# A graph layer on one core: the first group's second layer moved ahead, and the last three node blocks in an order written by hand

## The chip, the cores and the metric

The kernel runs on one core of a Trainium2 chip. The metric is the device time of one execution in microseconds (us), as the median of several runs. A core has five engines with a queue each: TensorE (PE, with its weight loads as PEld), VectorE (DVE), ScalarE (ACT), GpSimd (POOL) and SyncE (SP), which here only issues transfers.

## The reference, cut to what matters

There are 6250 nodes with 128 features and 100,000 edges, sorted by destination. Each edge passes a network of three layers, the messages are averaged over each node's incoming edges, each node passes a network of two layers, and the result is normalized.

```python
msg_in = concatenate([x[src], x[dst]], axis=-1)              # 100000 x 256
h = relu(msg_in @ Wm1 + bm1)                                 # 256 hidden
h = relu(h @ Wm2 + bm2)
messages = h @ Wm3 + bm3                                     # 128
agg = segment_sum(messages, dst) / clip(count, 1.0)[:, None]
upd = relu(concatenate([x, agg], axis=-1) @ Wn1 + bn1) @ Wn2 + bn2
y = x + (x + upd)
out = (y - mean(y)) / sqrt(var(y) + 1e-5)                    # over the 128 features
```

## The kernel before

The work has three stages. In all of them the arithmetic is in float32 (the destination half of the first edge layer is held as three bfloat16 terms).

**Tables (to about 84 us).** The products of all nodes with the two halves of `Wm1` are written to tables in DRAM, one half for sources (`atab`), one for destinations (`btab`). `x_part` (lines 316 to 320) computes the node features' own share of the later node layer, per block of 512 nodes as two products `c = 1, 0` of 512 columns, and lets ScalarE or VectorE empty each bank with the bias added. Blocks 9 and 12 are kept back for the edge stage (`X_FIRST`); block 12 is the short one, 106 nodes.

**Edges (84 to about 1129 us).** The loop runs over 196 groups of 512 edges (the last is shorter). For group g, POOL gathers rows of `atab` by source (`ag`, line 412, four buffers), SP loads windows of `btab` (`bw`, line 418), and

- `first_layer` (lines 449 to 460): TensorE transposes the gathered rows into two PSUM banks `ph` (tile pool `p1`, two buffers) and adds the destination share by a product with a 0/1 matrix `oht`, which VectorE compares out of the destinations (line 433); ScalarE applies bias and ReLU to both banks in four steps and so makes `h1`.
- `second_layer` (lines 469 to 471): sixteen matmul records on `h1` into two banks `ph2` (pool `p2`, two buffers), each emptied by VectorE with a `max` into `h2`. The products of `x_part` in this stage use the same two banks of `p2`.
- `sums` and `add_up` (lines 478 to 494): the sums by destination within a group are added to `acc` in SBUF.

One turn of the loop issues, for the group g that is due: `add_up` of group g - 4, `first_layer` of g, in the first two turns also the tests of the next group (`make_hot`) and one block of `x_part`, then `sums` of g - 3 and `second_layer` of g - 1. The order on TensorE is the order of the program (`manual_schedule`), and for the first six turns of the loop that of VectorE and ScalarE is too. So TensorE's order at the start of the stage is: first layer 0, block 9, first layer 1, block 12, second layer 0, first layer 2, second layer 1.

**Nodes (1131 us to the end).** The nodes are cut into 15 blocks: the last 106 nodes first, then blocks of 512, and at either end two of 256. `products` (line 671) multiplies `acc` by `Wm3` and POOL divides by the counts. `hidden` (lines 685 to 687) makes the hidden layer `u`. `norm` (lines 698 to 723) multiplies by `Wn2` into `pot` (two banks), adds twice the features, loaded by SP into `x2`, to give `y` (line 703, two buffers), takes the moments of each 128 nodes with `bn_stats` and `bn_aggr` (lines 707 and 708), the root on ScalarE (`sd`, 710), the reciprocal and the shift on VectorE (`rs` 712, `sh` 714), and scales `y` to `o` on ScalarE, 128 nodes an instruction (718). SP stores `o`. Blocks run four ahead for `products` and two behind for `norm`. TensorE's order is that of the program; VectorE's and ScalarE's order is a scheduler's.

Of the kernel before, what the change touches and what calls it, by code (L numbers as in the profile page):

```python
# [9 lines left out]
F32 = mybir.dt.float32  # L10
BF16 = mybir.dt.bfloat16
I32 = mybir.dt.int32
AF = mybir.ActivationFunctionType
ALU = mybir.AluOpType
AX = mybir.AxisListType
ENG = mybir.EngineType
# [3 lines left out]
P = 128  # L20
# [7 lines left out]
def kernel(  # L28
# [36 lines left out]
    nc = tc.nc  # L65
    N, D = x.shape
# [5 lines left out]
    NG = -(-E // GE)  # L72
# [78 lines left out]
    with tc.tile_pool(name="prep", bufs=1) as prep, tc.tile_pool(  # L151
        name="brow", bufs=6
    ) as brow, tc.tile_pool(name="pp", bufs=3, space=PSUM) as pp, tc.tile_pool(
        name="pb", bufs=5, space=PSUM
# [240 lines left out]
    with edge, tc.tile_pool(name="wk", bufs=2) as wk, tc.tile_pool(  # L395
        name="p1", bufs=2, space=PSUM
# [135 lines left out]
        for i in range(NG + ahead + 1):  # L532
            if i == 6:
                turns.close()
            if i == 16:
                late_loads()
                none = wk.tile([16, (NG * GE - E) // 16], I32, name="none", bufs=1)
                nc.vector.memset(none, NONE)
                nc.sync.dma_start(dpad[:E].rearrange("(p e) -> p e", p=16), dst.rearrange("(p e) -> p e", p=16))
                nc.sync.dma_start(dpad[E:].rearrange("(p e) -> p e", p=16), none)  # L540
            for step, after in enumerate((20, 24, 27)):
                if i >= after and (i - after) % 8 == 0 and (i - after) // 8 < len(pieces):
                    double((i - after) // 8, step)
            if i < NG:
                nt = GT if i < NGF else LT
                firsts = load_bases(tilei[0:1, i * GT:(i + 1) * GT], nt, ENG.SP)
                if i == NGF:
                    dbs = last_destinations()
                elif i % 2 == 0:
                    dbs = early.pop(0) if early else destinations(i, min(2, NGF - i), dst_row)  # L550
                st[i] = dict(nt=nt, got=fetch(srcT[:, i, :], nt, firsts), db=dbs.pop(0))
            g = i - ahead
            if 0 <= g < NG:
                s = st[g]
                ag, bw = s.pop("got")

                def make_hot(g):
                    s = st[g]
                    hots[g], s["oh"] = hot(s.pop("db"), pbase[:, g, :], dloc[:, g, :s["nt"]], s["nt"])

                if g not in hots:
                    make_hot(g)
                oht = hots.pop(g)
            k = g - lag - 1
            if 0 <= k < NG:
                s = st.pop(k)
                if "firsts" not in s:
                    s["firsts"] = load_bases(tilei[0:1, k * GT:(k + 1) * GT], s["nt"], ENG.DVE)
                add_up(s["part"], s["firsts"], s["nt"])
            if 0 <= g < NG:  # L570
                s = st[g]
                s["h1"] = first_layer(ag, bw, oht, s["nt"])
                if first:

                    make_hot(g + 1)
                    whole(x_part(first.pop(0), bank_p2, (nc.scalar, nc.vector)))
            k = g - lag
            if 0 <= k < NG:
                s = st[k]
                s["part"] = sums(s["oh"], s["h2"], s["nt"])  # L580
            m = g - 1
            if 0 <= m < NG:
                s = st[m]
                s["h2"] = h2s[m % NH2]
                second_layer(s["h1"], s["h2"], s["nt"])
# [59 lines left out]
    with tc.tile_pool(name="nd", bufs=2) as nd, tc.tile_pool(name="nr", bufs=1) as nr, tc.tile_pool(  # L645
        name="pm", bufs=4, space=PSUM
    ) as pm, tc.tile_pool(name="pu", bufs=2, space=PSUM) as pu, tc.tile_pool(
        name="po", bufs=2, space=PSUM
    ) as po, tc.manual_schedule(engines={ENG.PE}):


        rcol = nr.tile([P, NC], F32, name="rcol")
        nc.sync.dma_start(rcol, acc[0:1, HC, :NT * P].rearrange("o (p n) -> o p n", n=NC))
        nc.vector.tensor_scalar_max(rcol, rcol, 1.0)
        nc.vector.reciprocal(rcol, rcol)
        nc.sync.dma_start(rtab.rearrange("(p n) -> p n", n=NC), rcol)
        rrow = rtab.rearrange("(o n) -> o n", o=1)

        def products(b):

            n0, n1 = nodes_of[b]
            w = n1 - n0
            rc = nd.tile([P, NB], F32, name="rc", bufs=6)
            if b < SELF:
                nc.vector.tensor_scalar_max(rc[:, :w], acc[:, HC, n0:n1], 1.0)  # L665
                nc.vector.reciprocal(rc[:, :w], rc[:, :w])  # L666
            else:
                nc.sync.dma_start(rc[:, :w], rrow[:, n0:n1].to_broadcast([P, w]))
            pmt = pm.tile([P, NB], F32, name="pmt")
            for c in range(HC):  # L670
                nc.tensor.matmul(pmt[:, :w], w3[:, c, :], acc[:, c, n0:n1], start=(c == 0), stop=(c == HC - 1))  # L671
            total = nd.tile([P, NB], F32, name="total", bufs=3)
            nc.vector.scalar_tensor_tensor(total[:, :w], acc[:, HC, n0:n1], b23, pmt[:, :w],  # L673
                                           op0=ALU.mult, op1=ALU.add)
            agg = nd.tile([P, NB], F32, name="agg", bufs=5)
            nc.gpsimd.tensor_mul(agg[:, :w], total[:, :w], rc[:, :w])  # L676
            return agg

        def hidden(b, agg):
            n0, n1 = nodes_of[b]  # L680
            w = n1 - n0
            u = nd.tile([P, HC, NB], F32, name="u", bufs=4)
            for c in range(HC):
                put = pu.tile([P, NB], F32, name="put")
                nc.tensor.matmul(put[:, :w], wu1[:, 1, c * P:(c + 1) * P], agg[:, :w], start=True, stop=True)  # L685
                nc.vector.tensor_add(u[:, c, :w], put[:, :w], xu[c][:, n0:n1])  # L686
                nc.scalar.activation(u[:, c, :w], u[:, c, :w], AF.Relu)  # L687
            return u

        def norm(b, u):  # L690
            n0, n1 = nodes_of[b]
            w = n1 - n0
            k = -(-w // P)
            r = min(P, w)
            pot = po.tile([P, 4, D], F32, name="pot")
            for i in range(k):
                for c in range(HC):
                    nc.tensor.matmul(pot[:r, i, :], u[:, c, i * P:i * P + r], wu2[:, c, :],  # L698
                                     start=(c == 0), stop=(c == HC - 1))
            x2 = nd.tile([P, 4, D], F32, name="x2", bufs=3)  # L700
            nc.sync.dma_start(x2[:r, :k], x2tab[n0:n1, :].rearrange("(t p) d -> p t d", p=r))
            y = nd.tile([P, 4, D], F32, name="y")
            nc.vector.tensor_add(y[:r, :k, :], x2[:r, :k, :], pot[:r, :k, :])  # L703
            st = nd.tile([P, 4, 6], F32, name="st")
            mv = nd.tile([P, 4, 2], F32, name="mv")
            for i in range(k):
                nc.vector.bn_stats(st[:r, i, :], y[:r, i, :])
                nc.vector.bn_aggr(mv[:r, i, :], st[:r, i, :])
            sd = nd.tile([P, 4], F32, name="sd")
            nc.scalar.activation(sd[:r, :k], mv[:r, :k, 1], AF.Sqrt, bias=eps[:r])  # L710
            rs = nd.tile([P, 4], F32, name="rs")
            nc.vector.reciprocal(rs[:r, :k], sd[:r, :k])  # L712
            sh = nd.tile([P, 4], F32, name="sh")
            nc.vector.scalar_tensor_tensor(sh[:r, :k], mv[:r, :k, 0], -1.0, rs[:r, :k],  # L714
                                           op0=ALU.mult, op1=ALU.mult)
            o = nd.tile([P, 4, D], F32, name="o")
            for i in range(k):
                nc.scalar.activation(o[:r, i, :], y[:r, i, :], AF.Identity, bias=sh[:r, i:i + 1],  # L718
                                     scale=rs[:r, i:i + 1])
            if r == P:  # L720
                nc.sync.dma_start(out[n0:n1, :].rearrange("(t p) d -> p t d", p=P), o[:, :k, :])
            else:
                nc.sync.dma_start(out[n0:n1, :], o[:r, 0, :])

        B = len(nodes_of)
        FORE, BACK = 4, 2
        aggs = {b: products(b) for b in range(FORE)}
        us = {}
        for b in range(B + BACK):
            if b < B:  # L730
                us[b] = hidden(b, aggs.pop(b))
            if b >= BACK:
                norm(b - BACK, us.pop(b - BACK))
            if b + FORE < B:
                aggs[b + FORE] = products(b + FORE)


# [27 lines left out]
```

## Time and profile before

| | |
|---|---|
| median of 3 runs | 1210.17 us (1209.64 to 1211.73) |
| the profiled execution | 1208.8 us |
| its span | 1207.0 us |
| TensorE busy | 1178.5 us, 98% of the span |
| POOL, VectorE, ScalarE busy | 804.9, 670.4, 454.5 us |
| mean granted TensorE clock | 0.996 |
| first group's transposes start | 84.06 us |
| last matmul starts, last scaling starts | 1197.0 us, 1203.6 us |

The span runs from the first to the last instruction that the profiler recorded; the execution's own time lies 1.8 us above it. A row of the timeline merges neighbouring instructions of a kind and gives the start, the time from the first start to the last end, the engine, the line, the operation, the tile written and the tiles read, and in brackets the idle time of the engine before it with what ended it. An instruction's recorded duration includes its way through the engine, so the next one often starts before it ends.

### The profile page before, as it was taken

To read this page: it belongs to the slowest core of one execution; us is meant where nothing else is said; L and a number is where in the kernel's file an instruction comes from. 1 tells how busy PE (TensorE), PEld (TensorE's weight loads), DVE (VectorE), ACT (ScalarE), POOL (GpSimd) and SP (SyncE) were. 2 spreads that over 40 slices of the span, in tenths; PEclk is the share of its full clock that TensorE was granted. 3 is DMA by queue.
4 is the path that set the end of the run, shared out by engine and by line. 5 is a ranking of instruction groups with operands and counts; after the bars stand their busy time and mean duration, and the time that the engine had idled before them with its cause. 6 is when DMAs were issued, how large, how long until landed. Compare 5 with 4: busy or idle time off the path is not lost. (4 is left out here: it accounts for less than half of the span.)

```text
span 1207.0 us, 32797 instructions
## 1 busy us (share of the span) xinstructions
PE 1178.5 (98%) x11196; PEld 895.0 (74%) x11197; DVE 670.4 (56%) x2080; ACT 454.5 (38%) x1163; POOL 804.9 (67%) x859
## 2 busy tenths in 40 slices
PE   7989999999999999999999999999999999999896
PEld 6747777777777777777777777777777777777565
DVE  5864555555555555555555555555555555555586
ACT  5663333333333333333333333333333333333256
POOL 8267777777777777777777777777777777673220
PEclk9999999999999999999999999999999999999999
DMA  8886666666555555555555555555555555552343
GB/s 279 293 261 174 189 180 183 189 191 177 154 151 146 152 153 153 150 152 153 149 148 152 154 154 150 149 152 146 152 153 153 152 152 150 146 148 63 97 111 105
DMA packets 173672, 193.66 MB, mean 160 GB/s; under 512 B 30844, under 2 KB 145486, under 8 KB 173488
## 3 DMA queue, kind: packets, MB, share of 16 engines
q0 software_dynamic: 37984, 103.35, 31.1%
q1 hardware_dynamic: 106956, 61.93, 17.7%
q10 hardware_dynamic: 28564, 26.27, 8.1%
q8 instruction: 90, 1.47, 0.5%
q14 instruction: 78, 0.64, 0.2%
HBM read 168.92 MB, written 22.88 MB: 159 GB/s over the span
## 5 line engine op out<-in xcount | busy, mean ns | idle before, releaser
L412 POOL DMA_INDIRECT ag<-atab,srcT x784 | 752.8, 960 | 282.4 <-issue 184.3
L469 PE MATMUL ph<-w,h 128*128 128x256 f32 x3128 | 727.5, 386 | 1.0 <-ACT x_sb L318 1.0
L469 PEld LDWEIGHTS ph<-w,h 128*128 128x128 f32 x3128 | 578.1, 190 | 152.2 <-DVE acc L494 68.2
L460 ACT ACTIVATE h<-ph,b 128x256 f32<-128x256 f32 x782 | 306.3, 474 | 675.9 <-PE ph L455 495.3
L471 DVE TENSOR_TENSOR h<-ph,nb 128x512 f32<-128x512 f32 x391 | 270.2, 692 | 413.6 <-PE ph L469 411.1
L494 DVE TENSOR_TENSOR acc<-acc,pt 128x63 f32 x782 | 171.7, 220 | 33.9 <-PE ph L455 2.6
L449 PE MATMUL ph<-ident,ag 64*128 64x64 f32 x3128 | 130.3, 223 | 0.6 <-DVE b L382 0.6
L478 PE MATMUL pg<-h,oh 128*32 128x257 f32 x1564 | 125.6, 392 | 0.0
L449 PEld LDWEIGHTS ph<-ident,ag 64*128 64x128 f32 x3128 | 113.5, 139 | 2.7 <-ACT x_sb L318 1.4
L433 DVE TENSOR_SCALAR oht<-db,pbase 128x128 bf16<-128x128 int32 x392 | 104.9, 341 | 1.3 <-PE ph L455 1.0
L489 PEld LDWEIGHTS pt<-ident,part 64*128 64x128 f32 x1173 | 50.9, 136 | 65.9 <-issue 65.2
L455 PE MATMUL ph<-oht,bw 64*128 64x128 bf16 x1564 | 76.6, 217 | 2.7 <-DMA bw<-btab 2.3
L481 ACT COPY part<-pg 128x257 f32<-128x257 f32 x196 | 76.5, 390 | 4.0 <-PE pg L478 4.0
L489 PE MATMUL pt<-ident,part 64*128 64x64 f32 x1173 | 77.8, 238 | 0.2 <-DVE acc L494 0.2
L436 DVE TENSOR_TENSOR oh<-iota_n,dloc 128x128 f32<-128x128 f32 x196 | 55.0, 280 | 20.6 <-PE pg L478 19.7
L676 POOL TENSOR_TENSOR agg<-total,rc 128x512 f32<-128x512 f32 (+2 forms) x15 | 16.0, 1070 | 69.1 <-DVE total L673 65.1
L455 PEld LDWEIGHTS <-bw 64*128 64x128 bf16 x1564 | 53.6, 96 | 3.3 <-DMA bw<-btab 2.6
L232 PE MATMUL pbt<-w,xT 128*128 128x256 f32 x196 | 48.7, 394 | 2.5 <-ACT bt L241 1.6
L478 PEld LDWEIGHTS pg<-h,oh 128*32 128x32 f32 x1564 | 30.8, 108 | 21.7 <-issue 0.8
L232 PEld LDWEIGHTS pbt<-w,xT 128*128 128x128 f32 x196 | 36.8, 197 | 10.9 <-ACT bt L241 2.8
L252 POOL CAST bt<-rest 128x512 bf16<-128x512 f32 x18 | 12.2, 686 | 27.1 <-DVE rest L250 18.0
L698 PEld LDWEIGHTS pot<-wu,u 128*128 128x128 f32 (+1 forms) x196 | 24.0, 191 | 5.5 <-issue 4.8
(109 smaller groups left out, 418.2 us busy)
## 6 DMA issues: line engine op xcount, KB each, us to landing
bw<-btab SPq DMA_DIRECT2D x782, 32.0 KB
db<-in_dst_dram ACTq DMA_DIRECT2D x194, 128.0 KB
ag<-atab,srcT POOLq DMA_INDIRECT x784
btab<-bt SPq DMA_DIRECT2D x24, 384.0 KB
atab<-bt SPq DMA_DIRECT2D x24, 256.0 KB
xd<-in_x_dram SPq DMA_DIRECT2D x12, 256.0 KB
x2tab<-xd SPq DMA_DIRECT2D x12, 256.0 KB
x_sb<-in_x_dram SPq DMA_DIRECT2D x5, 512.0 KB
```

What stands on the lines that cost most here:

```text
L232: nc.tensor.matmul(pbt[:, a, :], xT[:, (t0 + a) * P:(t0 + a + 1) * P], w1[:, k, :], start=True, stop=True)
L412: nc.gpsimd.indirect_dma_start(out=ag[:, j, :], out_offset=None, in_=atab[:, :], in_offset=bass.IndirectOffsetOnAxis(ap=idx[:, j:j + 1], a ...
L433: nc.vector.tensor_scalar(oht[:n, k, :], db[:n, k * P:(k + 1) * P], pb_cols[:n, k:k + 1], None, op0=ALU.is_equal)
L449: nc.tensor.matmul(phs[h][:, c, u * NQ:(u + 1) * NQ], ag[halves[h], u, c * P:(c + 1) * P], ident[halves[h], halves[h]], is_transpose=True, ...
L455: nc.tensor.matmul(phs[h][:, c, k * P:(k + 1) * P], bw[halves[h], k, c * P:(c + 1) * P], oht[halves[h], k, :], start=False, stop=True, ski ...
L460: nc.scalar.activation(h1[:, c, h * 2 * P:(h + 1) * 2 * P], phs[h][:, c, :], AF.Relu, bias=b1[:, c:c + 1])
L469: nc.tensor.matmul(ph2[:, a, :], h1[:, c, (j0 + a) * P:(j0 + a + 1) * P], w2[:, c, :], start=(c == 0), stop=(c == HC - 1))
L471: nc.vector.tensor_tensor(h2[:, j0:j0 + 2, :H], ph2, nb2.to_broadcast([P, 2, H]), op=ALU.max)
L478: nc.tensor.matmul(pg[j * WN:(j + 1) * WN, :], oh[:, j, :], h2[:, j, :], start=True, stop=True, skip_group_check=True)
L481: nc.scalar.copy(part[:n, :], pg[:n, :])
L489: nc.tensor.matmul(pt[:, c, :], rows, ident[halves[h], halves[h]], is_transpose=True, start=True, stop=True, skip_group_check=True)
L494: nc.vector.tensor_add(window, window, pts[j // 2][:, :, k:k + WB])
```

## The change

There are two edits.

In the edge loop, the second layer of group 0 is issued in the turn of group 0 itself, behind the product of block 9; in the next turn it isn't issued again. TensorE's order becomes: first layer 0, block 9, second layer 0, first layer 1, block 12, first layer 2, second layer 1. VectorE's two `max` operations for it move ahead of the tests for group 2. From there on the order is as before.

In the node stage, `norm` is cut into `moments`, `deviation` (the root) and `scaled`. For the blocks up to the twelfth (index 11) they are called one after the other as before. For the last three blocks (12, 13, 14) VectorE and ScalarE follow the order of the program: moments and root of the next block are issued ahead of the scaling of the block before, and some of the scalings go to VectorE as `tensor_scalar` with two operands of one value a partition: the fourth 128 nodes of block 12, the second of block 13, the first of block 14. The tiles `y`, `mv`, `sd` and `o` get three buffers in place of two.

In the changed program VectorE's order from block 12's `y` on is: `y` of 12, `rs` of 11, first `bn_stats` of 12, `sh` of 11, the rest of 12's moments with each `bn_aggr` directly behind its `bn_stats`, `y` and moments of 13, `rs`, `sh` and a scaling of 12, `y` and moments of 14, `rs`, `sh` and a scaling of 13, the same of 14. ScalarE's is: scaling of 11, root of 12, root of 13, three scalings of 12, root of 14, one scaling of 13, one of 14. The order of SP and POOL is unchanged; the stores of the three blocks wait for both engines.

```diff
-            m = g - 1
-            if 0 <= m < NG:
+
+            m = g - 1 if g else g
+            if 0 <= m < NG and "h2" not in st[m]:
                 s = st[m]
                 s["h2"] = h2s[m % NH2]
                 second_layer(s["h1"], s["h2"], s["nt"])
...
-        def norm(b, u):
+        def moments(b, u):
...
-            y = nd.tile([P, 4, D], F32, name="y")
+            y = nd.tile([P, 4, D], F32, name="y", bufs=3)
...
-            mv = nd.tile([P, 4, 2], F32, name="mv")
+            mv = nd.tile([P, 4, 2], F32, name="mv", bufs=3)
             for i in range(k):
                 nc.vector.bn_stats(st[:r, i, :], y[:r, i, :])
                 nc.vector.bn_aggr(mv[:r, i, :], st[:r, i, :])
-            sd = nd.tile([P, 4], F32, name="sd")
+            return y, mv
+
+        def deviation(b, mv):
...
+            sd = nd.tile([P, 4], F32, name="sd", bufs=3)
             nc.scalar.activation(sd[:r, :k], mv[:r, :k, 1], AF.Sqrt, bias=eps[:r])
+            return sd
+
+        def scaled(b, y, mv, sd, engines):
...
-            o = nd.tile([P, 4, D], F32, name="o")
-            for i in range(k):
-                nc.scalar.activation(o[:r, i, :], y[:r, i, :], AF.Identity, bias=sh[:r, i:i + 1],
-                                     scale=rs[:r, i:i + 1])
+            o = nd.tile([P, 4, D], F32, name="o", bufs=3)
+            for i, eng in zip(range(k), engines):
+                if eng is nc.scalar:
+                    eng.activation(o[:r, i, :], y[:r, i, :], AF.Identity, bias=sh[:r, i:i + 1], scale=rs[:r, i:i + 1])
+                else:
+                    eng.tensor_scalar(o[:r, i, :], y[:r, i, :], rs[:r, i:i + 1], sh[:r, i:i + 1],
+                                      op0=ALU.mult, op1=ALU.add)
...
+        for b in range(B - 1):
+            us[b] = hidden(b, aggs.pop(b))
             if b >= BACK:
-                norm(b - BACK, us.pop(b - BACK))
+                y, mv = moments(b - BACK, us.pop(b - BACK))
+                scaled(b - BACK, y, mv, deviation(b - BACK, mv), [nc.scalar] * 4)
             if b + FORE < B:
                 aggs[b + FORE] = products(b + FORE)
+
+        assert BACK == 2
+        with tc.manual_schedule(engines={ENG.DVE, ENG.Activation}):
+            us[B - 1] = hidden(B - 1, aggs.pop(B - 1))
+            ends = [(B - 3, [nc.scalar, nc.scalar, nc.scalar, nc.vector]), (B - 2, [nc.scalar, nc.vector]),
+                    (B - 1, [nc.vector, nc.scalar])]
+            before = None
+            for b, engines in ends:
+                y, mv = moments(b, us.pop(b))
+                sd = deviation(b, mv)
+                if before:
+                    scaled(*before)
+                before = b, y, mv, sd, engines
+            scaled(*before)
```

## The prediction

> **What bounds the kernel now.** I read the page's first two parts, then the timeline around the two places that the diff touches, the chain of the last 17 us, and the granted clock by stretch. First the page:
>
> ```profile
> span 1207.0 us, 32797 instructions
> PE 1178.5 (98%) x11196; PEld 895.0 (74%) x11197; DVE 670.4 (56%) x2080; ACT 454.5 (38%) x1163; POOL 804.9 (67%) x859
> PE   7989999999999999999999999999999999999896
> ```
>
> TensorE is busy from slice 3 to slice 38, so nothing is to be had between: a gain must come from the head, where TensorE waits, or from the tail, where it has finished. The edits touch one of each. The timeline of the head (start, us, what; in brackets the idle time before and what ended it):
>
> ```profile
> 87.80 2.63 PE L316 MATMUL ph<-xT,wu 128*128 128x512 f32 x4
> 87.91 1.57 ACT L460 ACTIVATE h<-ph,b 128x256 f32<-128x256 f32 x4 [4.88 <-PE ph L455]
> 89.35 0.70 ACT L318 ACTIVATE x_sb<-ph,bu 128x512 f32<-128x512 f32 x1
> 90.36 1.11 PE L449 MATMUL ph<-ident,ag 64*128 64x64 f32 x16
> 91.83 0.96 PE L316 MATMUL ph<-xT,wu 128*128 128x106 f32 x4
> 93.37 0.37 ACT L318 ACTIVATE x_sb<-ph,bu 128x106 f32<-128x106 f32 x1
> 93.79 3.72 PE L469 MATMUL ph<-w,h 128*128 128x256 f32 x16 [1.01 <-ACT x_sb L318]
> 97.45 0.72 PE L449 MATMUL ph<-ident,ag 64*128 64x64 f32 x16
> 98.31 3.72 PE L469 MATMUL ph<-w,h 128*128 128x256 f32 x16
> ```
>
> Group 0's second layer (93.79) waits 1.01 us for ScalarE to empty the bank of the small product at 91.83. That wait is what the first edit can remove. From 98.31, the second layer of group 1, both orders are alike, so that start is the yardstick. The clock in stretches (the number before the DMA share is the granted TensorE clock):
>
> ```profile
> 86.00:88.00 2.00, 0.80 (x9) 0.47 (x10) 0.00 (x0) 0.09 (x1) 1.39 (x3) 1.00 0.73 200
> 88.00:90.00 2.00, 2.00 (x4) 0.47 (x3) 0.00 (x0) 2.00 (x5) 1.70 (x2) 0.75 0.84 225
> 90.00:92.00 2.00, 2.00 (x26) 1.45 (x26) 1.34 (x4) 0.12 (x2) 1.39 (x3) 0.50 0.54 158
> 92.00:94.00 2.00, 0.99 (x5) 0.82 (x6) 0.33 (x1) 1.74 (x5) 1.65 (x2) 0.90 0.59 160
> ```
>
> After a stretch in which TensorE waited for transfers the clock is halved, from 89.0 to 92.4 (shares missing: 0.5 of the time at half from 88 to 90, all of it to 92, 0.2 of it to 94, 3.4 us together). The tail's timeline:
>
> ```profile
> 1192.23 0.69 DVE L703 TENSOR_TENSOR y<-x,pot 128x512 f32<-128x512 f32 x1 [0.24 <-issue]
> 1195.34 0.69 DVE L703 TENSOR_TENSOR y<-x,pot 128x512 f32<-128x512 f32 x1 [0.56 <-ACT o L718]
> 1196.50 1.65 ACT L718 ACTIVATE o<-y,sh,rs 128x128 f32<-128x128 f32 x4 [0.70 <-ACT u L687]
> 1198.18 0.42 DVE L703 TENSOR_TENSOR y<-x,pot 128x256 f32<-128x256 f32 x1 [0.83 <-ACT o L718]
> 1200.76 0.42 DVE L703 TENSOR_TENSOR y<-x,pot 128x256 f32<-128x256 f32 x1 [1.34 <-ACT o L718]
> 1203.19 0.88 ACT L718 ACTIVATE o<-y,sh,rs 128x128 f32<-128x128 f32 x2 [0.48 <-DVE sh L714]
> ```
>
> Each `y` of blocks 12, 13 and 14 (1195.34, 1198.18, 1200.76) waits for ScalarE to finish the scaling `o` two blocks earlier, because `y` has two buffers. VectorE and ScalarE work in turn, and the chain of these 17 us gives the scaling 35% of them.
>
> **The sum, against 1208.8 us.** The profiled execution took 1208.8 us, 1.8 us around its span of 1207.0; the median of the three runs, 1210.17, is 1.4 us above it. I take the difference that I work out off the median.
>
> *Tail.* A third buffer for `y`, `mv` and `sd` and the new order. (1) Block 12's `y` then waits for its products alone. These start at 1192.84 and 16 take 1.95 us; block 11's `y` came 0.09 us after its products. So 1194.88, where it was 1195.34, and VectorE is free by then (1194.78). From `y` of block 12 to block 11's scaling it was 1.16 us, so that runs from 1196.04 to 1197.7. (2) In the order written by hand each `bn_aggr` stands right behind its own `bn_stats` and waits for it. The rows show 0.03 us from an end to a dependent start, 0.26 to 0.29 for `bn_stats`, and 0.08 from an aggregation to the next start: 0.37 a pair, against 0.26 when they are staggered. Block 12's moments are then ready 2.36 us after its `y` starts (2.01 before), at 1197.24. (3) There block 13's `y` starts, 0.94 us sooner than before. 0.42 for it, two pairs and the gaps: moments at 1198.56. (4) On ScalarE block 13's root is queued ahead of block 12's scaling, which therefore can't start before 1198.8. On VectorE block 12's reciprocal and shift (0.17 and 0.16, each with 0.03 behind it) end at 1198.85. Three tiles on ScalarE (1.26 by the chain's row of three) run from 1198.9 to 1200.2; the fourth goes to VectorE. No 128x128 scaling on VectorE is in the trace. The nearest rows are a `tensor_scalar` 128x106 at 0.22, 128x256 at 0.29, and 0.67 for the same beside a running POOL instruction; POOL is through by 1185 in the tail. I take 0.25, bounds 0.22 and 0.67. (5) Block 14's `y` at 1199.16, moments 1.32 later at 1200.48, root to 1200.80, while VectorE does block 13's reciprocal, shift and one tile to 1201.05. Then reciprocal and shift of block 14 to 1201.36, and its last tile on ScalarE from 1201.44 for 0.49: 1201.93. Before, the last scaling ended at 1203.19 + 0.88 = 1204.07. Gain 2.1 us. The 128 KB of the last store follow, as before, with 2.9 us from its issue to the end of the span; the three last stores come 0.6 to 1.2 us apart instead of 1.5 and more, and the transfer rate of the tail's rows (over 300 GB/s) needs 0.4 us for one of them, so I add nothing, at most 0.4. With the price of the VectorE scaling at its upper end twice on the path, and the stores, the gain is 0.9; if half of the 0.11 us that each of the eight pairs loses is hidden, it is 2.6.
>
> The three stores now wait for both engines; nothing stands behind them on SP. The third `o` buffer relaxes waits for stores long landed. The 15 us of node blocks before the tail stay bound by TensorE products.
>
> *Head.* The order becomes: product of block 9, second layer 0, group 1's products, small product, group 2's, second layer 1. Sixteen matmuls move, with two VectorE `max` operations, and no DMA of their own. The removed wait is 1.0 to 1.2 us (the small product's last start and 0.1 behind it give 92.6; the wait ends at 93.79). What is late next: group 2's products write the two banks that ScalarE reads for group 1's `h1`. ScalarE ends that 1.03 + 1.57 us after the products start (97.45 and 98.48 show the 1.03), but TensorE gets there after 0.87 (97.45 to 98.31) and some 0.55 for the small product. That is a new wait of 1.2 us. Second layer 0 itself must wait for block 9's evacuation, 89.35 + 0.70 = 90.05, and TensorE is there at 90.2 with the halved clock: no wait. So one wait takes the other's place. The halved 2 us after 90.36 now hold second-layer matmuls, which lose 1.0 us, instead of group 1's products (1.47 until the next start, 0.87 at full clock) and the small one (0.3 lost): 0.1 more. In this phase of the clock the head costs +0.1. If the clock is whole, TensorE reaches second layer 0 at 89.5 and waits 0.6 for block 9's evacuation, against a wait removed that is 0.3 longer: +0.3. If the halved stretch lies some 2 us earlier, the product of block 9 is slow throughout, hides that evacuation entirely, and the head gains 0.4. I take 0.1 gained, the middle, with both ends for the range. Group 5's gathers are held back by 2.7 us, as they wait for group 1's products to free their buffer; they are needed at 113.2 and now issued by 100.4, so this costs nothing; without the 13 us of cover it would be the 2.7 us. The SP loads for the same group have the same cover, and VectorE's tests for group 2, now behind two `max`, are needed at 98.
>
> A rule on the clock: the Trainium skill, "TensorE: Matmul & The Clock Gate", section "What's actually happening", has a free-running window of 3413 ns, which the 3.4 us of the rows match. The section "Why this matters for your kernels" of that page of the Trainium skill wants idle gaps above about 3 us before the clock falls; here two gaps of 1.1 and 1.2 us with one matmul between were enough, so the row decides. By the page's rule no such gap is in either order, the head would be +0.3 and the time 1208.4.
>
> Sum: -2.1 - 0.1 = -2.2, so 1210.17 - 2.2 = 1208.0 us.
>
> **Rivals.** *The head gains too* (1206.0 to 1207.7): the halved stretch falls where the new order gains 0.4, or the new order fills a stretch that would otherwise be halved a second time, worth half of 3.4, 1.7 us. For it: the idle time of 84.8 to 87.3 is shared, and dense second-layer matmuls now follow it directly. Against: the new wait before group 2's products is as long as the old. *The tail gives half* (1208.7 to 1209.3): the VectorE scaling costs 0.67, or the bunched stores queue. Against: POOL is idle there. *A second halved stretch* (slower): group 1's products, small product, a 1.2 us wait and group 2's products now stand in a row, 3.7 us with little dense work; the stretch that brought the fall had about as little. Each halved stretch costs 1.7 us; one leaves the total at -0.5, and from the second on it is slower, 1211.4.
>
> **How the numbers follow.** A difference of 0.2%, 2.4 us, is about what a measurement of this kernel can tell from none; the bound lies at 1207.75, hard by the forecast. Forecast 0.64, own range 1207.4 to 1208.9, of it 0.30 below the bound and 0.34 above; the head gains too 0.22, all faster; half a tail, or one more halved stretch, 0.08, same; two of them 0.06, slower. Faster 0.52, same 0.42, slower 0.06. The range 1206.1 to 1209.5 leaves out the slower case and the edges of the others.
>
> **What would show it.** Block 12's `y` 0.09 us behind its products, no `y` released by an `o`; the last scaling ending 9.7 us after block 11's `y` starts (11.8 before); block 12's scaling released late, behind block 13's root. In the head: second layer 0 directly behind block 9's product, and group 2's products released by ScalarE after about 1.2 us. Wrong: a `y` still released by ScalarE; a VectorE scaling above 0.4 us; second layer 1 starting more than 0.5 us from 98.3 with the same halved stretch.

## The result, and the profile after

The changed kernel took 1207.26 us in the median of 22 runs (1204.68 to 1209.94), the kernel before 1211.18 us in 22 runs beside it (1207.43 to 1212.65). The ratio, taken from the means (1207.45 and 1210.71), is 0.9973 with a 95% interval of 0.9966 to 0.998: 3.3 us less, 2.4 to 4.1; the medians lie 3.9 us apart. Differences given below from ratios are these times 1210 us. The interval lies below 1, with its upper end on the bound of 0.2% that the prediction took: faster. One execution among those of the experiments, of the kernel before with a late doubling, took 2345.05 us and is left out of its ratio.

The forecast had the direction and the range; its gain, 2.2 us, lies 0.2 us short of the interval's lower end. Its time, 1208.0 us, lies closer to 1207.26 than the gain does, because the kernel before came out at 1211.18 us here and at 1210.17 in the three runs that the forecast started from; that part is luck.

The profiled execution of the changed kernel took 1206.23 us around a span of 1204.5 us. Start of the page:

```profile
span 1204.5 us, 32804 instructions
PE 1179.8 (98%) x11196; PEld 896.4 (74%) x11197; DVE 672.3 (56%) x2083; ACT 454.0 (38%) x1160; POOL 804.4 (67%) x859
PE   7999999999999999999999999999999999999997
```

ScalarE has three instructions fewer and VectorE three more, the three scalings that changed engine. TensorE is as full as before. Where the span's 2.5 us went, from the starts in the two timelines (each is rounded, so the sum is out by some hundredths):

| stretch | before | after | difference |
|---|---|---|---|
| to group 0's first transpose | 84.06 | 83.69 | -0.37 |
| from there to second layer 1 (the head) | 14.25 | 12.77 | -1.48 |
| from there to block 11's `y` | 1093.92 | 1095.25 | +1.33 |
| from there to the end of the last scaling (the tail) | 11.83 | 9.75 | -2.08 |
| from there to the end of the span | 2.97 | 3.00 | +0.03 |

The tail is the forecast's. The head and the long middle each moved by more than a microsecond, in opposite directions, and that is what the experiments are mainly about.

The tail in the timeline of the changed kernel (line 705 is `y`, 709 and 710 the moments, 717 the root, 728 the shift, 733 a scaling on ScalarE, 735 one on VectorE):

```profile
1191.71 0.69 DVE L705 TENSOR_TENSOR y<-x,pot 128x512 f32<-128x512 f32 x1
...
1194.36 0.69 DVE L705 TENSOR_TENSOR y<-x,pot 128x512 f32<-128x512 f32 x1
...
1195.56 0.26 DVE L709 BATCH_NORM_STATS2 st<-y 128x6 f32<-128x128 f32 x1
...
1195.86 0.18 DVE L710 BATCH_NORM_AGGREGATE mv<-st 128x2 f32<-128x6 f32 x1
1195.96 0.26 DVE L709 BATCH_NORM_STATS2 st<-y 128x6 f32<-128x128 f32 x1
...
1196.74 0.40 DVE L705 TENSOR_TENSOR y<-x,pot 128x256 f32<-128x256 f32 x1
...
1198.18 0.29 ACT L717 ACTIVATE sd<-mv,eps 128x2 f32<-128x2 f32 x1 [0.77 <-DVE rs L726]
1198.18 0.16 DVE L728 SCALAR_TENSOR_TENSOR sh<-mv,rs 128x4 f32<-128x4 f32 x1
1198.38 0.34 DVE L735 TENSOR_SCALAR o<-y,rs,sh 128x128 f32<-128x128 f32 x1
1198.38 1.26 ACT L733 ACTIVATE o<-y,sh,rs 128x128 f32<-128x128 f32 x3
1198.64 0.41 DVE L705 TENSOR_TENSOR y<-x,pot 128x256 f32<-128x256 f32 x1
...
1200.97 0.49 ACT L733 ACTIVATE o<-y,sh,rs 128x128 f32<-128x128 f32 x1 [0.20 <-ACT o L733]
```

No `y` has a bracket any more, so none waits for an `o`, and the alternation of the two engines is gone. The head:

```profile
86.27 3.34 PE L316 MATMUL ph<-xT,wu 128*128 128x512 f32 x4
...
89.45 3.62 PE L469 MATMUL ph<-w,h 128*128 128x256 f32 x16
...
93.00 0.71 PE L449 MATMUL ph<-ident,ag 64*128 64x64 f32 x16
...
93.86 0.69 PE L316 MATMUL ph<-xT,wu 128*128 128x106 f32 x4
...
95.23 1.07 PE L449 MATMUL ph<-ident,ag 64*128 64x64 f32 x16 [0.67 <-ACT h L460]
...
96.46 3.72 PE L469 MATMUL ph<-w,h 128*128 128x256 f32 x16
```

Second layer 0 (89.45) follows block 9's product directly, and group 2's transposes (95.23) now wait for ScalarE. The granted clock in stretches (the number before the DMA share):

```profile
84.00:86.00 2.00, 0.84 (x21) 0.54 (x18) 1.07 (x6) 0.00 (x0) 1.62 (x2) 0.91 0.58 167
86.00:88.00 2.00, 2.00 (x7) 0.91 (x4) 0.00 (x0) 1.32 (x4) 1.46 (x2) 0.50 0.75 170
88.00:90.00 2.00, 2.00 (x6) 1.02 (x5) 0.29 (x1) 0.93 (x2) 1.40 (x2) 0.74 1.10 235
```

The halved stretch is as long as before, 3.4 us, but runs from 85.6 to 89.0 where it ran from 89.0 to 92.4. It lies over block 9's product, no longer over group 1's products.

### The profile page after: what moved, and what is told of

Same layout as the page of the kernel before. It is cut to its first block, busy times and chain, and to the rows that moved or that the text cites. A ratio compares the mean times of both kernels' runs of the same rounds, so it can differ in the third digit from the quotient of the medians.

```text
span 1204.5 us, 32804 instructions
## 1 busy us (share of the span) xinstructions
PE 1179.8 (98%) x11196; PEld 896.4 (74%) x11197; DVE 672.3 (56%) x2083; ACT 454.0 (38%) x1160; POOL 804.4 (67%) x859
## 3 DMA queue, kind: packets, MB, share of 16 engines
q8 instruction: 90, 1.47, 0.5%
```

## The experiments

Two theories on the tail: the third buffers, the hand order and VectorE's share each give what the timeline prices them at (mine); or the stores or VectorE's scaling take back part of it. Three on the head: one wait for another, worth nothing (mine); a gain of its own; a loss by further halved stretches.

**The two edits apart.** Only the edge loop's edit (`m = g - 1 if g else g`, and the test for `"h2"`):

> The kernel before with the first edit alone: group 0's second layer directly behind the product of block 9. Theory 1 (one wait for another, as in the prediction): -0.4 to +0.3 us against the kernel before, by the place of the halved stretch of the clock. Theory 2 (the head gains more than the prediction took, since the new order has fewer or better covered stretches at half clock): -0.8 to -1.8 us, and runs with a higher mean granted clock than those of the kernel before. Theory 3 (the tail is worth more than its profile shows): 0 here, within 0.3 us.

Only the node stage's edit:

> The kernel before with the second edit alone: the last three blocks in the order written by hand, with three buffers. All theories that trust the two profiles: -2.1 us, 1.8 to 2.4, last scaling ending 9.75 us after block 11's y starts. Theory 3 (the tail is worth more than its profile shows): -3 us or more.

The first edit alone took 1210.94 us against 1210.70: ratio 0.9999, 0.999 to 1.0008, so nothing, within 1.2 us. The second alone took 1208.34: ratio 0.9979, 0.9969 to 0.9989, 2.5 us less (1.3 to 3.8), with a tail of 9.74 us. So the gain that can be told is the tail's. In the profile of the first edit alone the head is no shorter:

```profile
84.87 0.28 PE L455 MATMUL ph<-oht,bw 64*128 64x128 bf16 x1 [1.05 <-DMA bw<-btab]
86.35 0.29 PE L455 MATMUL ph<-oht,bw 64*128 64x128 bf16 x2 [1.20 <-DMA bw<-btab]
...
87.25 3.78 PE L316 MATMUL ph<-xT,wu 128*128 128x512 f32 x4
90.82 3.97 PE L469 MATMUL ph<-w,h 128*128 128x256 f32 x16
...
96.95 1.07 PE L449 MATMUL ph<-ident,ag 64*128 64x64 f32 x16 [0.67 <-ACT h L460]
```

Both waits for the destination windows `bw` stand at their full length here, and the clock was halved from 84.7 to 91.5, 6.8 us, two stretches on end (the first and the last two-microsecond window of it, the clock again ahead of the DMA share):

```profile
84.00:86.00 2.00, 0.28 (x1) 0.10 (x1) 0.49 (x3) 0.00 (x0) 1.39 (x3) 0.67 0.56 148
...
90.00:92.00 2.00, 2.00 (x6) 1.32 (x5) 0.75 (x1) 0.04 (x1) 1.36 (x2) 0.62 0.55 165
```

The second begins at 88.1, ahead of the first instruction that the edit moves on TensorE (90.82), so I don't put it to the edit.

**The head with TensorE kept busy.** Six products of `w1` with itself that nothing reads are added as filler: four in group 0's first layer between the transposes and the destination share, and two where each order waits for ScalarE. Both kernels have the node stage of before.

```diff
+        def fill(n):
+            if n:
+                dm = pa.tile([P, H + 1], F32, name="pg")
+                for _ in range(n):
+                    nc.tensor.matmul(dm[:, :H], w1[:, 0, :P], w1[:, 0, :], start=True, stop=True)
...
+            fill(4 if oht is warm.get("first") else 0)   # first_layer of group 0, ahead of the bw products
...
+                fill(2 if m == 0 else 0)                 # kernel before: ahead of second layer 0
+                fill(2 if g == 2 else 0)                 # first edit: ahead of group 2's first layer
```

The kernel before with the filler:

> The kernel before with six idle products of 128x128 by 256 that nothing reads, into a free bank, about 0.43 us each: four in group 0's first layer ahead of the destination share, where TensorE waits for transfers, two ahead of group 0's second layer, where it waits for ScalarE. They keep the array busy and change no order. Theory 2 (the clock makes the head): the halved stretch near 89 us is gone in the profile, and the time falls by 0.8 to 1.8 us. Theory 1: by at most the halved stretch itself, 1.7 us, less what the products hold up; the order's own worth shows only in the pair with the next run.

The first edit with the filler:

> The same six idle products with the first edit: four at the same place, two ahead of group 2's first layer, where the new order waits for ScalarE. Against the run before it, theory 1: +0.3 us, the price of the order at whole clock. Theory 2: the same, +0.3 or 0, as the clock is whole in both, so that the gain of the first edit alone is gone. A third way, that the order saves waits for transfers: -0.5 us or more here too.

Before with filler took 1208.61 us (0.9989, 0.9978 to 1.0), the first edit with filler 1207.61 (0.9974, 0.9965 to 0.9983: 3.1 us less, 2.1 to 4.2). With TensorE busy the first edit is worth about 1.5 us (the means of their 11 runs each, 1209.21 and 1207.66, differ by 1.55, standard error 0.5). Theories 1 and 2 had 0 to +0.3 us for this pair; only the third way, that the order saves waits for transfers, had a gain. The timelines of TensorE suggest how. Before with filler (line 464 is the destination share here, 478 the second layer, 449 the filler):

```profile
90.33 0.23 PE L464 MATMUL ph<-oht,bw 64*128 64x128 bf16 x2 [0.88 <-DMA bw<-btab]
91.86 0.34 PE L464 MATMUL ph<-oht,bw 64*128 64x128 bf16 x5 [1.30 <-DMA bw<-btab]
...
93.60 5.25 PE L478 MATMUL ph<-w,h 128*128 128x256 f32 x16
```

The first edit with filler:

```profile
86.08 1.98 PE L316 MATMUL ph<-xT,wu 128*128 128x512 f32 x4
88.38 3.72 PE L478 MATMUL ph<-w,h 128*128 128x256 f32 x16 [0.32 <-ACT x_sb L318]
...
92.58 0.39 PE L464 MATMUL ph<-oht,bw 64*128 64x128 bf16 x8
92.90 0.69 PE L316 MATMUL ph<-xT,wu 128*128 128x106 f32 x4
93.43 1.05 PE L449 MATMUL pg<-w 128*128 128x256 f32 x4
```

In the old order TensorE now meets group 1's windows too early, at 90.33 and 91.86, and the clock is halved at 93.5 instead, over second layer 0 (5.25 us for 3.72). In the new order the second layer lies in front of those windows: group 1's eight products run without a wait, and there is no halved stretch in this head at all. So in this pair of profiles the early second layer hides a transfer, for a TensorE that is early enough to wait for it. Without filler most of that time has already gone to group 0's windows. That this is where the 1.5 us come from is read from one profile of each kernel and not tested apart. In these two profiles the heads take 15.76 and 12.78 us, more apart than the times are: the runs of before with filler spread from 1206.65 to 1212.57, so not every execution need meet both waits in full. One more thing differs: with filler and the first edit the scheduler issues the first load of the features (see below) a turn earlier. It doesn't make the pair's difference in these profiles: from second layer 1 to the first product of the node stage they take 1033.16 and 1033.26 us.

**The tail by steps.** Only the four `bufs=3`, in the order of the scheduler:

> The kernel before with a third buffer for y, mv, sd and o and nothing else; the scheduler orders VectorE and ScalarE. If the gain of the second edit comes from the y that no longer wait for the scaling two blocks earlier: most of it, -1.4 us, with 10.4 us from block 11's y to the end of the last scaling (11.84 before, 9.75 after). If it comes from the order written by hand: 0 to -0.5 us, 11.4 us or more.

The node stage's edit with all scalings on ScalarE (`ends = [(B - 3, [nc.scalar] * 4), (B - 2, [nc.scalar] * 2), (B - 1, [nc.scalar] * 2)]`), the edge loop as before:

> The second edit alone, but with all scalings left on ScalarE. By the rows of after (0.39 us a scaling on ScalarE, a block's root queued ahead of the scaling): 10.1 us from block 11's y to the end, 0.35 longer than with VectorE's three scalings, -1.75 us against the kernel before. If VectorE's share is what makes the edit, it is over 11 us.

The changed kernel with each `bn_aggr` one `bn_stats` late in the last three blocks:

```diff
-            for i in range(k):
-                nc.vector.bn_stats(st[:r, i, :], y[:r, i, :])
-                nc.vector.bn_aggr(mv[:r, i, :], st[:r, i, :])
+            late = 1 if b >= B - 3 else 0
+            for i in range(k + late):
+                if i < k:
+                    nc.vector.bn_stats(st[:r, i, :], y[:r, i, :])
+                if i >= late:
+                    nc.vector.bn_aggr(mv[:r, i - late, :], st[:r, i - late, :])
```

> After, with each bn_aggr of the last three blocks one bn_stats behind, as in the scheduler's order. The prediction priced the wait of each pair at 0.11 us, eight pairs; the trace of after shows 0.40 us a pair against 0.26. If VectorE's chain sets the end throughout: 0.7 us off the 9.75, to about 9.1. If ScalarE's queue (block 12's scaling behind block 13's root) does: less than 0.3.

| tail | block 11's `y` to end of last scaling | ratio to before |
|---|---|---|
| before | 11.83 us | |
| third buffers alone | 10.36 | 0.9989 (0.998 to 0.9998) |
| hand order, ScalarE alone | 10.03 | 0.9989 (0.998 to 0.9998) |
| the edit, with VectorE's share | 9.74 | 0.9979 (0.9969 to 0.9989) |
| both edits, pairs staggered | 9.02 | 0.9964 (0.9951 to 0.9977) |

Every step shortens the tail. Most of it, 1.47 us, is the buffers'. With them alone VectorE stands idle ahead of no `y` of the last three blocks, and the stretch runs from the first of these rows to the end of the second:

```profile
1194.51 0.69 DVE L703 TENSOR_TENSOR y<-x,pot 128x512 f32<-128x512 f32 x1
...
1203.99 0.88 ACT L718 ACTIVATE o<-y,sh,rs 128x128 f32<-128x128 f32 x2 [0.48 <-ACT sd L710]
```

The shares hold for this order of adding; the hand order without the third buffers was not run. Staggering the pairs gives back what the hand order lost, 0.73 us (0.7 was expected if VectorE's chain sets the end throughout). The staggered timeline for block 13:

```profile
1199.76 0.40 DVE L707 TENSOR_TENSOR y<-x,pot 128x256 f32<-128x256 f32 x1
1200.20 0.49 DVE L713 BATCH_NORM_STATS2 st<-y 128x6 f32<-128x128 f32 x2
1200.60 0.30 DVE L715 BATCH_NORM_AGGREGATE mv<-st 128x2 f32<-128x6 f32 x2
1200.85 0.18 DVE L731 RECIPROCAL rs<-sd 128x4 f32<-128x4 f32 x1
```

From `y` to the reciprocal 1.09 us, where the changed kernel has 1.26 (1196.74 to 1198.00). The ratios of whole runs don't contradict this order, but they can't tell neighbours in the table apart, and the first two are the same.

**The best version.** The changed kernel with the stagger and the filler of the head:

> The run before it with the six idle products of the filled runs at the head. If the order's worth at the head shows only where the clock is whole and the transfers are late, as the filled pair suggests, this adds 1 to 3 us to the gain of the run before it: -5 us against the kernel before. If the fill only pays back what it costs: within 0.7 us of the run before it.

It took 1204.79 us (1204.15 to 1205.48): ratio 0.9949, 0.9936 to 0.9963, 6.2 us less than before (4.5 to 7.7). By the ratios that is 1.8 us more than without the filler, within the 1 to 3 expected, though the two intervals overlap. It beats both kernels, with six products more than either.

**Where the middle lost its time.** Two places carry the +1.33 us of the first table. One is a halved stretch at 1130 us, at the start of the node stage: from the first product of `products` to block 11's `y` it is 60.8 to 60.9 us in the three profiles without it (before, the second edit alone, before with filler) and 61.4 to 61.6 us in the eleven with it, so some 0.6 us. The other is the turn at group 6, 6.05 us in place of 5.27. VectorE and TensorE of the changed kernel there:

```profile
117.17 0.22 DVE L494 TENSOR_TENSOR acc<-acc,pt 128x63 f32 x1
...
120.83 0.69 DVE L518 SCALAR_TENSOR_TENSOR xd<-xd,bu 128x512 f32<-128x512 f32 x1 [3.44 <-DMA xd<-in_x_dram]
121.44 0.54 DVE L494 TENSOR_TENSOR acc<-acc,pt 128x63 f32 x2
...
122.53 0.36 PE L489 MATMUL pt<-ident,part 64*128 64x64 f32 x5 [0.48 <-DVE acc L494]
```

The doubling of the features for the node stage (`xd`) waits 3.44 us for its load; the additions to `acc` stand behind it on VectorE, and TensorE waits for them. Before, `xd` waited 2.60 us, and TensorE not at all:

```profile
121.86 0.69 DVE L518 SCALAR_TENSOR_TENSOR xd<-xd,bu 128x512 f32<-128x512 f32 x1 [2.60 <-DMA xd<-in_x_dram]
```

I tried to take this away by issuing the doubling two turns later, in the kernel before and in the first edit alone:

```diff
-            for step, after in enumerate((20, 24, 27)):
+            for step, after in enumerate((20, 26, 29)):
```

> The kernel before with the doubling of the features (VectorE, line 518) and its store two turns of the loop later; the load (line 516) stays. In the traces of after and of the first edit alone VectorE stands 3.4 us at the first of these operations, for its load, and TensorE waits 0.5 to 1.3 us behind it, near 122 us; in the trace of before that wait held up nothing. Theory of the give-back: little here, 0 to -0.8 us against the kernel before.

> The first edit alone with the doubling two turns later. If what the new order gains at the head is given back near 122 us, since the load there is issued by SP at its own pace: the loss is gone, and this is 0.8 to 1.5 us faster than the run before it and than the first edit alone (which measured no difference). If the head's order is worth nothing: within 0.4 us of the run before it.

and in the second edit alone and in both:

> The second edit alone with the doubling two turns later: the tail's 2.1 us and what the later doubling gives, -2.1 to -2.9 us against the kernel before; 9.75 us from block 11's y to the last scaling.

> After with the doubling two turns later. Give-back theory: 0.8 to 1.5 us faster than the run before it, -3.4 to -4.2 us against the kernel before, and no wait of TensorE between 100 and 150 us but the 0.3 us for the tests of group 3. Otherwise as after, -3.3, and within 0.4 of the run before it.

The four medians were 1210.10, 1209.90, 1207.56 and 1207.80 us: ratios 0.999 (0.998 to 1.0001), 0.9994 (0.9985 to 1.0002), 0.9976 (0.9965 to 0.9987) and 0.9976 (0.9967 to 0.9985). The 0.8 to 1.5 us expected of the first edit did not appear. VectorE's timeline of the first edit with the late doubling shows that the edit didn't do what it says:

```profile
118.45 0.22 DVE L494 TENSOR_TENSOR acc<-acc,pt 128x63 f32 x1
122.81 0.69 DVE L518 SCALAR_TENSOR_TENSOR xd<-xd,bu 128x512 f32<-128x512 f32 x1 [4.13 <-DMA xd<-in_x_dram]
123.41 0.54 DVE L494 TENSOR_TENSOR acc<-acc,pt 128x63 f32 x2
```

The doubling stands between the same additions as before. From the seventh turn on VectorE's order is the scheduler's, which put the operation back where it had been. So these four runs don't test the theory; what they give is two more pairs on the head.

That the load's landing sets this wait is read from the profiles. A load lands in 16 parts; in the thirteen profiles that have all of them on record, the last one lies 0.10 us or less ahead of the doubling. In twelve of the fourteen profiles the load is issued 18.4 to 18.7 us after second layer 1 and the doubling starts 23.6 to 25.1 us after it; what this exceeds 23.6 is, to 0.1 us, what the turn is longer (24.37 in the changed kernel, 0.78 longer). In the other two, the new order with filler, the scheduler put the load behind 36 loads of windows in SP's order, where the other kernels have 40, so it is issued a turn earlier, at 15.6 and 16.2 us; the doubling waits 0.48 and 0.32 us for it, and the turn isn't longer. Nobody planned that, but it agrees with the theory: with the load a turn earlier the loss in this turn is gone. From issue to the last part the load takes 5.1 to 6.0 us in the old order, 5.6 to 6.6 in the new one without filler, and 3.2 and 3.9 in these two. Why it lands late, and later in the new order, is open.

## Why the prediction was right, and where it was short

**Tail, step by step.** (1) Block 12's `y` was to come 0.09 us behind its products and to wait for no `o`: so it is. (2) A pair of `bn_stats` and `bn_aggr` was priced at 0.37 us: it is 0.40 (1195.56 to 1195.96), 0.03 more each. (3) Block 13's `y` was due 2.36 us after block 12's, block 14's 4.28: measured 2.38 and 4.28. Eight pairs of 0.03 us would be 0.2 us more; the gaps around them were priced too long by nearly as much, so it is partly luck that the whole fits to 0.05 us. (4) Block 12's scaling was due 4.02 us after its `y`, and started there, at 1198.38. ScalarE had begun block 13's root 0.20 us earlier, and VectorE's shift ended at 1198.34, so it was the shift that came last, as in the working, and the root's place ahead of it cost nothing. (5) VectorE's scaling, priced at 0.25, is recorded with 0.34 and 0.35 us, but the next instruction starts 0.26 us after it (1198.38 to 1198.64), and on the path that counts. (6) The stores added nothing: 3.0 us from the last scaling to the end in both. The whole was to take 9.7 us and took 9.75. The rival "the tail gives half" is out.

**Head.** The new wait was put at 1.2 us. From the small product's start to second layer 1 it is 2.60 us in the changed kernel; the first edit's filled run shows 0.53 from that product to the next start (92.90 to 93.43), and group 2's undelayed products take 0.87, so 1.20. That it replaces the old one holds. Three cases were priced by where the halved stretch lies; the profiles without filler hold two of them. From block 9's product to second layer 1:

| profile | order | clock halved within | us |
|---|---|---|---|
| before | old | 3.41 (from 89.0) | 10.52 |
| before, late doubling | old | 3.29 | 10.88 |
| second edit | old | 2.65 | 11.41, of it 0.89 lost to group 1's windows |
| second edit, late doubling | old | 2.78 | 10.63 |
| third buffers | old | 4.89 | 11.56 |
| hand order, ScalarE alone | old | 5.67 | 11.67 |
| both edits | new | 2.76 (to 89.0) | 10.18 |
| first edit | new | 4.28 | 10.93 |
| both, late doubling | new | 4.54 | 11.05 |
| first edit, late doubling | new | 5.09 | 11.32 |
| both, staggered | new | 5.84 | 11.69 |

The new order's rows lie on a line, 8.87 us and 0.48 for each halved microsecond. At 3.41 that is 10.51, what the old order takes in the phase of the kernel before: no difference, where a cost of 0.1 was forecast. Where the stretch lies earlier, over block 9's product, the new order is ahead, for the same halved time, by 0.1 to 0.4 us (11.59 by the line against 11.67, 10.20 against 10.63), the forecast's bound of 0.4. A whole clock was seen in no head without filler, so the case priced at +0.3 stays open; its wait for block 9's evacuation, put at 0.6 us, is 0.32 in the first edit's filled run. In the profiles the term held in mechanism and size; the times of whole runs bound it only to about 1.2 us either way.

**What the sum lacked** is what happens outside the yardstick. The prediction said that both orders are alike from second layer 1 on. In the profiles they are not: in the seven old-order ones the turn at group 6 takes 0.5 us more than 5.27 in the mean (0 to 0.9), in the five new-order ones without filler 1.1 more (0.8 to 1.4). That is of the size of the head's gain, with the opposite sign, and the times of whole runs show neither: four pairs with and without the first edit (differences of the ratios, times 1210 us) give -0.1 (alone), -0.7 (with the second edit), +0.5 and 0.0 us (the same with the late doubling), -0.1 in the mean. Four pairs with and without the second edit give -2.5, -3.1, -1.7 and -2.2, -2.4 in the mean. Their sum, -2.5 us, is 0.3 from the forecast. (It is the mean of two differences between both edits and none: -3.3 us, and -1.7 with the late doubling in both.) That the loss at group 6 cancels the head's gain is thus a reading of the profiles; each pair's interval is about 1 us or more to either side, too wide to show the one or the other.

**The rest of the -3.3.** The other run of both edits, with the late doubling, gave -2.9 (1.8 to 4.0). In the profile of the changed kernel 1.2 us of the head's 1.48 come from group 0's windows, which were waited for 2.33 us before (1.13 and 1.20) and 1.15 now (1.00 and 0.15). These products stand ahead of everything that the edit moves on TensorE, and the first edit alone waited 2.43 us for them, so I count this to the execution, not to the change. What is left between -2.5 and -3.3 lies inside the interval, and its cause is not settled.

**The rivals.** The median lies 0.1 us below the forecast's own range and within the times given for "the head gains too", yet that rival's mechanism isn't shown: halved stretches over block 9's product did occur, and no pair of runs shows their worth. With filler the head did gain more, about 1.5 us, and what the profiles suggest for it, the transfer for group 1, wasn't in the rival. "A second halved stretch" did come in four of the five new-order profiles without filler and in two of six old-order ones without it, but it began ahead of the moved work (at 88.1 us against 90.82 in the first edit alone), not behind group 1's products, where the rival put it; the first edit alone, with two stretches in its profile, was as fast as before.

**The clock.** The profiles show halved stretches of 3.41 and 6.83 us. They match one and two of the windows of 3413 ns that the Trainium skill gives in "TensorE: Matmul & The Clock Gate", section "What's actually happening". The page's section "Why this matters for your kernels" warns of idle gaps above about 3 us. Here the longest gap in any of these heads is 1.37 us, gaps of about 1 us were followed by a halved clock, and where the filler took those of group 0 away, the halving at 85 to 92 us was gone. The rows decide, as the prediction took it.

## What to carry to other kernels

Where two engines work in turn at the end of a kernel, look first for the buffer that ties them: it gave 1.5 of the 2.1 us here, the hand order and the second engine 0.3 each, and setting the two operations of each dependent pair one place apart 0.7 more. A wait removed on a busy engine is worth only what the next late thing leaves, so follow the order past the point where it looks the same again, to the next operation that waits for a transfer with others behind it. And see on the engine that an edit of the program's order did move the instruction, before reading the time as an answer.

## What the hardware showed that was not expected

- Products that nothing reads made the kernel faster: six of them, about 3 us of TensorE, in gaps of about 1 us. With the first edit and the old tail the profile's head has no halved clock, and the kernel took 3.1 us less than before (2.1 to 4.2); in the order of before the halved stretch moved to 93.5 us, and the kernel took 1.3 us less (0 to 2.7).
- With the new order and the filler the times also agreed better: the first edit's 11 runs have a standard deviation of 0.6 us, the best version's 5 runs 0.5; the kernels measured beside the first have 1.1 to 1.7, the 1.7 being the order of before with the same filler.
- A 128x128 `tensor_scalar` with two operands of one value a partition is recorded on VectorE with 0.34 to 0.35 us and lets the next one start after 0.26; the same scaling on ScalarE starts every 0.38 to 0.40 us (four in 1.65, one alone 0.49).
